# Dealing the modulation's products unevenly over the steps of a QR decomposition

## The chip, the cores and the metric

The kernel runs on one core of a Trainium2 chip. The metric is the device time of one execution in microseconds. Beside the timed runs there is one execution recorded by the hardware profiler; its span and the time lines below come from that one.

## What is computed

The input `x` has 8 samples of 512 tokens and 576 features, with one condition vector per sample. Two layers follow one another, all in float32.

```python
# layer 0: rotate each sample inside a 64-dimensional subspace
U, _ = jnp.linalg.qr(P)                       # P is 576 x 64
v = jax.nn.silu(cond) @ W.T + b               # entries of a skew 64 x 64 matrix A
R = expm(A)                                   # one per sample
z = jnp.einsum('btn,nd->btd', x, U)
x = x + jnp.einsum('btd,nd->btn', jnp.einsum('btd,bde->bte', z, R) - z, U)
# layer 1: a transformer block with modulation
ada = jax.nn.silu(c) @ ada_w + ada_b          # 8 x 3456
shift_msa, scale_msa, gate_msa, shift_mlp, scale_mlp, gate_mlp = jnp.split(ada, 6, axis=1)
x = x + gate_msa * attention(modulate(layernorm(x), shift_msa, scale_msa))
x = x + gate_mlp * mlp(modulate(layernorm(x), shift_mlp, scale_mlp))
```

The attention mixes the 16 heads of one token, and the MLP is 2304 wide.

## The kernel before

**The front of the kernel.** In the first 213 us the kernel makes the subspace, the rotations and the modulation. The QR of `P` is done by Householder steps, one for each of the 64 columns (`qr_step`, line 271, called from the loop at line 555). TensorE contributes two small products to each step: `rp` (line 274) broadcasts a row of the matrix, and `dp` (line 282) sums columns over the partitions. The rest of the step is a chain on VectorE: `sg` (line 291) reads `rp`, `w` (line 320) needs the norm `nrm` that ScalarE makes from `dp` (line 298), and then come the update of the matrix `m` (lines 327 and 337) and the products of the next column, `t` (lines 263 and 268). The next `rp` needs the updated `m`, and the next `dp` needs `t`.

**What is put beside it.** After each step (from the third on, line 558) the loop calls `next(side)` once. `side` is the generator `beside()` (line 528). Whatever it issues in that call stands in TensorE's queue behind the `dp` of this step and ahead of the `rp` of the next one. The order on TensorE, VectorE, ScalarE and GpSimd is the order in which the instructions are written here, since the stage has a manual schedule (line 164); SyncE's queue of DMAs is ordered by the scheduler.

`beside()` deals out three kinds of work:

- The entries of the skew matrices, `skew_entries` (line 399): eight groups of five products, four products per step, in steps 4 to 13.
- The modulation, `modulations()` (line 517): nine column blocks (`ada_columns`, line 360) of five products each (line 364, moving 384 columns over 8 rows of the condition), with a copy by ScalarE into `ada_rows` after each block (line 366) and the load of the block four further on. After blocks 1, 2, 5 and 7 a `modulation(v)` (line 371) transposes a part of `ada_rows` into `mod` by ten or twelve short products (lines 375 and 379) and ScalarE copies the result. A piece is what the generator does from one `yield` to the next: one column product, or one `modulation`; there are 49 pieces.
- The matrix exponential of all eight skew matrices, `expm` (line 445): the even and odd series by a few 64 x 64 products (`products`, line 424; eight per call, line 429), their sums on GpSimd, and 19 squarings of two `products` calls each, the last of one.

`expm` is itself a generator. In the version before it yields `True` or `False`: with `True`, `beside()` also takes one `next(rest)`, where `rest` is the modulation dealt in threes by `paced(3, ...)` (line 342); with `False` nothing is added. So steps 14 to 17 get three pieces each, then every step of the series gets three, the step with the products `hic` and `hin` (27) and the squarings (31 to 49) get none, and what is left follows in step 50.

```python
rest = paced(3, [modulations()])
...
for free in expm(*eyes):
    if free:
        next(rest, None)
    yield
for _ in rest:
    yield
```

When the generator's blocks 4 and 8 are complete, the gates are stored to DRAM by SyncE (line 369).

**Behind it.** From 213 us the triangular factor is inverted block by block, the first tile is rotated, and from then on the tiles go through qkv (line 821), attention on VectorE (lines 859 to 894), projection (line 957) and the MLP (lines 1001 to 1080).

Of the kernel before, what the change touches and what calls it, by code (L numbers as in the profile page):

```python
# [49 lines left out]
def rotate_then_dit_block(  # L50
# [113 lines left out]
    with tc.manual_schedule(engines=engines), tc.tile_pool(name="prep", bufs=1) as prep, tc.tile_pool(name="qrs", bufs=2) as qrs, tc.tile_pool(  # L164
# [177 lines left out]
        def paced(n, parts):  # L342

            k = 0
            for part in parts:
                for _ in part:
                    k += 1
                    if k % n == 0:
                        yield
# [6 lines left out]
        def load_ada(g):  # L356
            aws[g] = adap.tile([128, NK, AC], F32, tag="aw", name=f"aw_{g}")
            load_rows(aws[g], ada_w[:, g * AC : (g + 1) * AC], 65)

        def ada_columns(g):  # L360
            ps = ps_m.tile([B, AC], F32, tag="m", name=f"ada_{g}")
            for c in range(NK):
                k = srows(c)
                nc.tensor.matmul(ps, lhsT=sc[0:k, c, :], rhs=aws[g][0:k, c, :], start=c == 0, stop=c == NK - 1)  # L364
                yield
            nc.scalar.copy(ada_rows[:, g * AC : (g + 1) * AC], ps)
            for k in range(2):
                if g == (4, 8)[k]:
                    nc.sync.dma_start(out=gates_d[k], in_=ada_rows[:, (3 * k + 2) * D : (3 * k + 3) * D])

        def modulation(v):
            ps = ps_m.tile([128, NK, B], F32, tag="m", name=f"mod_{v}")
            for c, rows in enumerate(KROWS):
                first = v * D + c * 128
                nc.tensor.matmul(
                    ps[0:rows, c], lhsT=ada_rows[:, first : first + rows], rhs=ident[0:B, 0:B], start=True, stop=True
                )
            if v > 1:
                nc.tensor.matmul(
                    ps[64:128, 4],  # L380
                    lhsT=ada_rows[:, v * D + 512 : (v + 1) * D],
                    rhs=ident[0:B, 0:B],
                    start=True,
                    stop=True,
                )
            for c0, c1, rows in ((0, 4, 128), (4, 5, 128 if v > 1 else 64)):
                dst = mod[0:rows, v // 3 * 2 + v % 3, c0:c1, :]
                if v % 3:
                    nc.scalar.activation(dst, ps[0:rows, c0:c1], AF.Identity, bias=ones[0:rows, 0:1])
                else:  # L390
                    nc.scalar.copy(dst, ps[0:rows, c0:c1])
# [29 lines left out]
        def ex(tag):  # L421
            return exs.tile([128, B // 2, R], F32, tag=tag, name=f"ex_{tag}")

        def products(lhs, rhs, name):

            ps = ps_ex.tile([128, B // 2, R], F32, tag="ex", name=name)
            for b in range(B // 2):
                for p in (slice(0, R), slice(R, 128)):
                    nc.tensor.matmul(ps[p, b, :], lhsT=lhs[p, b, :], rhs=rhs[p, b, :], start=True, stop=True)
            return ps  # L430
# [14 lines left out]
        def expm(i1, i2, half):  # L445


            a, at_s = ex("a"), ex("at_s")
            nc.gpsimd.tensor_tensor(au, au, skew_mask.unsqueeze(1).to_broadcast([128, B // 2, R]), ALU.mult)
            yield True  # L450
            nc.scalar.copy(at_s, products(au, i1, "at"))
            nc.gpsimd.tensor_tensor(a, au, at_s, ALU.subtract)
            yield True
            yield True

            s1, s2, s3 = ex("s1"), ex("s2"), ex("s3")
            nc.scalar.copy(s1, products(a, a, "aa"))

            ns = prep.tile([128, B // 2], F32, tag="ns", name="ns")
            nan = prep.tile([128, B // 2], F32, tag="nan", name="nan")  # L460
            nc.vector.tensor_reduce(ns, a, AX.X, ALU.add, apply_absolute_value=True)
            nc.gpsimd.tensor_scalar(ns, ns, EXPM_LIMIT * 2.0**-N_SQUARINGS, None, ALU.is_ge)
            parts = {}
            for name, cs in (("c", COS_C), ("n", SIN_C)):
                lo, hi, tp = parts[name] = ex("lo" + name), ex("hi" + name), ex("tp" + name)
                nc.gpsimd.tensor_scalar(lo, s1, cs[1], None, ALU.mult)
                if name == "n":
                    nc.gpsimd.tensor_tensor(lo, lo, i1, ALU.add)
                nc.gpsimd.tensor_scalar(hi, i1, cs[3], None, ALU.mult)
            yield True  # L470
            nc.scalar.copy(s2, products(s1, s1, "ss"))
            ps = ps_m.tile([128, B // 2], F32, tag="m", name="over")
            nc.tensor.matmul(ps, lhsT=half, rhs=ns, start=True, stop=True)
            nc.scalar.copy(nan, ps)
            yield True
            nc.scalar.copy(s3, products(s1, s2, "sss"))
            for name, cs in (("c", COS_C), ("n", SIN_C)):
                lo, hi, tp = parts[name]
                for acc, s, c in ((hi, s1, cs[4]), (hi, s2, cs[5]), (lo, s2, cs[2])):
                    nc.gpsimd.tensor_scalar(tp, s, c, None, ALU.mult)  # L480
                    nc.gpsimd.tensor_tensor(acc, acc, tp, ALU.add)
            nc.gpsimd.tensor_scalar(nan, nan, 0.0, 3e38, ALU.is_gt, ALU.mult)
            nc.gpsimd.tensor_scalar(nan, nan, 3e38, 0.0, ALU.mult, ALU.mult)
            for _ in range(4):
                yield True
            for name in ("c", "n"):
                lo, hi, tp = parts[name]
                nc.scalar.copy(tp, products(s3, hi, "hi" + name))
                nc.gpsimd.tensor_tensor(lo, lo, tp, ALU.add)
            yield False  # L490
            yield True
            even, odd = parts["c"][0], parts["n"][0]
            e, f, e2, f2 = ex("e"), ex("f"), ex("e2"), ex("f2")
            sn = ex("sn")
            nc.scalar.copy(sn, products(a, odd, "sn"))
            nc.gpsimd.tensor_tensor(e, even, sn, ALU.subtract)
            nc.gpsimd.tensor_tensor(f, even, sn, ALU.add)
            nc.gpsimd.tensor_tensor(f2, f, i2, ALU.add)
            nc.gpsimd.tensor_tensor(e2, e, i2, ALU.add)
            yield True  # L500
            yield True

            for k in range(N_SQUARINGS):
                pair = [(e, e2, f2, f"pe_{k}"), (f, f2, e2, f"pf_{k}")]
                if k % 2:
                    pair.reverse()
                if k == N_SQUARINGS - 1:
                    pair = [x for x in pair if x[0] is f]
                made = [products(other, src, name) for src, _, other, name in pair]
                for (src, plus, _, _), ps in zip(pair, made):  # L510
                    nc.scalar.copy(src, ps)
                    if len(pair) == 2:
                        nc.gpsimd.tensor_tensor(plus, src, i2, ALU.add)
                yield False
            nc.gpsimd.tensor_tensor(fmi, f, nan.unsqueeze(2).to_broadcast([128, B // 2, R]), ALU.add)

        def modulations():

            for g in range(9):
                yield from ada_columns(g)  # L520
                if g + 4 < 9:
                    load_ada(g + 4)
                v = {1: 0, 2: 1, 5: 3, 7: 4}.get(g)
                if v is not None:
                    modulation(v)
                    yield

        def beside():
            yield
            yield  # L530
            yield from paced(4, [skew_entries(g) for g in range(8)])
            skew_rows()
            rest = paced(3, [modulations()])
            for _ in range(4):
                next(rest)
                yield
            for free in expm(*eyes):
                if free:
                    next(rest, None)
                yield  # L540
            for _ in rest:
                yield
# [8 lines left out]
        first_xt = xin.tile([128, D], F32, tag="xt", name="xt_0_0", bufs=2)  # L551
        eyes = identities()
        side = beside()
        t, done = column_products(0), None
        for j in range(R):
# [687 lines left out]
    for k, (b, ts) in enumerate(units):  # L1243
# [38 lines left out]
        s3s, rest = mlp(pr, gate_m, aside)  # L1282
# [58 lines left out]
```

## Time and profile before

| | |
|---|---|
| median of 3 runs | 2154.73 us |
| lowest and highest | 2151.36 and 2156.78 us |
| the profiled execution | 2156.77 us |
| its span, first to last instruction | 2155.1 us |
| TensorE busy | 2051.7 us, 95% |
| VectorE busy | 1818.1 us, 84% |
| GpSimd busy | 730.3 us, 34% |
| ScalarE busy | 432.9 us, 20% |
| chain that ended last | 75% on TensorE, 16% on VectorE |

Times in the profile are counted from the start of the span. The page has the span in 40 slices with the busy share of each engine in tenths and the TensorE clock that was granted, then the chain that ended last, then the groups of instructions by line. PE is TensorE, DVE is VectorE, ACT is ScalarE, POOL is GpSimd, SP is SyncE. In a timeline row stand the start, the time of the row, engine, line, operation, output and inputs, shapes, how many, and in brackets how long the engine was idle before and what ended that. In a row of waits stand the waiting instruction, the one that released it, the time in all, the number and the longest.

A step is counted here from one `sg` (line 291) to the next, with the first column as step 0. Step 14 begins at 56.6 us, step 17 at 66.3, step 27 at 107.1, step 31 at 124.8, step 50 at 181.7, and the last at 213.1.

### The profile page before, as it was taken

The numbers are of one execution on the slowest core, as the hardware profiler recorded it, in microseconds if no ns is written. First come the engines' busy times: TensorE is split into PE (matmuls) and PEld (weight loads), VectorE is DVE, ScalarE is ACT, GpSimd is POOL, SyncE is SP. The second block draws the span as 40 slices with busy tenths as digits, with TensorE's granted clock in tenths as the row PEclk, the third lists the DMA queues.
The fourth block names the chain that finished last, engine by engine and source line by source line (L and its number), as shares of the span: only waits on it lengthen the run. The fifth ranks groups of instructions, "written<-read, shape, count | busy, mean of one in ns | idle before, by whom it ended". The sixth has DMA issues, their size and how long they took to land.

```text
span 2155.1 us, 28246 instructions
## 1 busy us (share of the span) xinstructions
PE 2051.7 (95%) x10109; PEld 1621.1 (75%) x10109; DVE 1818.1 (84%) x2548; ACT 432.9 (20%) x1040; POOL 730.3 (34%) x959
## 2 busy tenths in 40 slices
PE   5996898999999999999999999999999999998998
PEld 3476666777878878887878787888878787776777
DVE  8898499799997988979797979798997999989821
ACT  2232222221211221222121121121121211111210
POOL 2331153241523333333333243323333434343322
PEclk9855799999999999999999999999999999999999
DMA  8202256375757666575748484756657676665564
GB/s 278 87 2 75 82 189 176 116 227 167 216 192 205 210 185 213 170 236 161 249 137 270 127 266 147 223 194 195 221 177 222 194 226 166 205 188 189 168 193 139
DMA packets 251456, 392.44 MB, mean 182 GB/s; under 512 B 86926, under 2 KB 139099, under 8 KB 251316
## 3 DMA queue, kind: packets, MB, share of 16 engines
q1 hardware_dynamic: 225396, 364.09, 54.9%
q10 hardware_dynamic: 25920, 26.55, 3.6%
q8 instruction: 80, 1.31, 0.2%
q14 instruction: 60, 0.49, 0.1%
HBM read 331.63 MB, written 58.94 MB: 181 GB/s over the span
## 4 chain that ended last, share of the span: by engine, by line
PE 75%; DVE 16%; issue 3%; POOL 2%; DMA 2%; ACT 2%; ACTq 0%; SPq 0%; POOLq 0%; DVEq 0%
PE fc L1001 25%; PE qkvp L821 15%; PE fc L1075 9%; PE fc L1080 6%; PE pj L957 5%; DVE sc L866 3%; PE fc L1077 3%; PE p L1106 2%; DVE qk L859 2%; PE ada L364 1%; PE rot L762 1%; PE zps L751 1%; DVE att L894 1%; DVE pv L887 1%; PE dp L282 1%
## 5 line engine op out<-in xcount | busy, mean ns | idle before, releaser
L1001 PE MATMUL fc<-h2T,w 128*128 128x256 f32 x2304 | 519.0, 381 | 3.4 <-ACT h2T L977 2.3
L821 PE MATMUL qkvp<-wqkv,hT 128*128 128x288 f32 (+1 forms) x1920 | 484.4, 409 | 7.5 <-ACT qs L832 5.3
L1001 PEld LDWEIGHTS fc<-h2T,w 128*128 128x128 f32 x2304 | 433.6, 191 | 70.9 <-ACT h2T L977 9.5
L821 PEld LDWEIGHTS qkvp<-wqkv,hT 128*128 128x128 f32 (+1 forms) x1920 | 363.0, 191 | 110.0 <-ACT qs L832 7.1
L859 DVE TENSOR_TENSOR qk<-qkv 128x2304 f32<-128x2304 f32 x128 | 336.7, 2631 | 4.2 <-ACT qkv L829 2.0
L887 DVE TENSOR_TENSOR pv<-sc,qkv 128x2304 f32<-128x2304 f32 x128 | 333.5, 2606 | 2.7
L894 DVE TENSOR_REDUCE att<-pv 128x144 f32<-128x2304 f32 x128 | 326.0, 2547 | 3.1
L866 DVE TENSOR_REDUCE sc<-qk 128x64 f32<-128x2304 f32 x128 | 326.2, 2548 | 2.5
L1100 POOL TENSOR_TENSOR s<-gt 128x128 f32<-128x128 f32 x144 | 88.9, 619 | 453.3 <-ACT gt L1022 453.3
L1022 ACT ACTIVATE gt<-fc,b 128x256 f32<-128x256 f32 x288 | 118.8, 471 | 610.1 <-PE fc L1001 575.2
L1075 PE MATMUL fc<-wq,gt 128*128 128x288 f32 x576 | 170.8, 417 | 9.9 <-ACT gt L1022 6.7
L1080 PEld LDWEIGHTS fc<-wt,ss 128*128 128x128 f32 x1152 | 161.2, 191 | 15.3
L1080 PE MATMUL fc<-wt,ss 128*128 128x144 f32 x1152 | 165.1, 287 | 0.0
L1033 POOL TENSOR_TENSOR x<-x,mt 128x288 f32<-128x288 f32 x64 | 71.6, 1120 | 227.3 <-DVE mt L1032 227.3
L832 ACT COPY qs<-qkvp 128x288 f32<-128x288 f32 x180 | 71.5, 397 | 378.4 <-PE qkvp L821 337.9
L1097 POOL TENSOR_TENSOR ss<-gt 128x128 f32<-128x128 f32 x144 | 116.9, 812 | 69.6 <-PE fc L1080 68.0
L1099 POOL TENSOR_TENSOR ss<-gt,ss 128x128 f32<-128x128 f32 x144 | 133.0, 924 | 10.0
L1075 PEld LDWEIGHTS fc<-wq,gt 128*128 128x128 f32 x576 | 99.4, 190 | 44.4 <-issue 15.6
L957 PE MATMUL pj<-w2q_p,aT 128*128 128x288 f32 x384 | 104.0, 406 | 2.9 <-DVE u L1137 1.6
L146 POOL TENSOR_TENSOR rstd_m<-rstd_m,mhalf 128x1 f32<-128x1 f32 x32 | 26.7, 835 | 222.1 <-DVE rstd_m L145 222.1
L1075 PE MATMUL fc<-wt,gt 128*128 128x288 f32 x288 | 93.9, 408 | 0.0
L1077 PE MATMUL fc<-wq,ss 128*128 128x288 f32 x288 | 93.9, 408 | 0.0
(265 smaller groups left out, 2379.9 us busy)
## 6 DMA issues: line engine op xcount, KB each, us to landing
w<-in_fc_w SPq DMA_DIRECT2D x288, 256.0 KB, 5.0
wq<-in_fc_q SPq DMA_DIRECT2D x144, 432.0 KB, 4.3
wt<-comb_d SPq DMA_DIRECT2D x144, 432.0 KB, 5.6
tok<-qs ACTq DMA_DIRECT2D x180, 144.0 KB, 1.8
qkv<-tok SPq DMA_DIRECT2D x30, 864.0 KB, 4.6
w2q_p<-in_proj_w SPq DMA_DIRECT2D x32, 432.0 KB, 4.0
xT<-in_x_t SPq DMA_DIRECT2D x16, 640.0 KB, 4.9
w1t<-in_fc_t SPq DMA_DIRECT2D x80, 128.0 KB, 4.4
```

Source lines behind the costliest of these rows:

```text
L821: nc.tensor.matmul(ps, lhsT=hT[0:k, c, i * 128 : (i + 1) * 128], rhs=wqkv[0:k, c, cols], start=c == 0, stop=c == NK - 1,)
L859: nc.vector.tensor_tensor(pr, q[:, c * HC : (c + 1) * HC].unsqueeze(2).to_broadcast([128, HC, H, DH]), k.unsqueeze(1).to_broadcast([128, H ...
L866: nc.vector.tensor_reduce(sc[t][:, c * HC : (c + 1) * HC, :], pr, AX.X, ALU.add)
L887: nc.vector.tensor_tensor(pr, sc[t][:, c * HC : (c + 1) * HC, :].unsqueeze(2).to_broadcast([128, HC, DH, H]), v.unsqueeze(1).to_broadcast( ...
L894: nc.vector.tensor_reduce(att[:, c * HC : (c + 1) * HC, :], pr, AX.X, ALU.add)
L957: nc.tensor.matmul(ps, lhsT=aT[0:k, c, :], rhs=w, start=c == 0, stop=c == NK - 1)
L1001: nc.tensor.matmul(bank[:, k], lhsT=lhs, rhs=h2T[rows, c, 0 : NU * 128], start=start, stop=stop, skip_group_check=True)
L1022: nc.scalar.activation(gt[:, k].rearrange("p t s -> p (t s)"), bank[:, k], AF.Gelu, bias=b1[:, 2 * g + k : 2 * g + k + 1])
L1075: nc.tensor.matmul(p[k], lhsT=whole[k][0], rhs=whole[k][1], start=g == 0, stop=stop)
L1077: nc.tensor.matmul(p[2], lhsT=whole[2][0], rhs=whole[2][1], start=g == 0, stop=stop)
L1080: nc.tensor.matmul(bank[:, side], lhsT=lhs, rhs=rhs[:, n * QUARTER : (n + 1) * QUARTER], start=False, stop=stop, skip_group_check=True,)
L1099: nc.gpsimd.tensor_tensor(ss[:, 2], gt[:, 1, 0], ss[:, 1], ALU.subtract)
```

## The change

`expm` now yields a number instead of a truth value, and `beside()` takes that many single pieces of the modulation in that step. Steps of the series without products yield 4, those with products 1, and the step with `hic` and `hin` and the squarings still 0. The first four steps take three pieces each as before. After `expm`, what is left is taken one piece at a time.

```diff
             a, at_s = ex("a"), ex("at_s")
             nc.gpsimd.tensor_tensor(au, au, skew_mask.unsqueeze(1).to_broadcast([128, B // 2, R]), ALU.mult)
-            yield True
+            yield 4
             nc.scalar.copy(at_s, products(au, i1, "at"))
             nc.gpsimd.tensor_tensor(a, au, at_s, ALU.subtract)
-            yield True
-            yield True
+            yield 1
+            yield 4
...
                 nc.gpsimd.tensor_scalar(hi, i1, cs[3], None, ALU.mult)
-            yield True
+            yield 1
             nc.scalar.copy(s2, products(s1, s1, "ss"))
...
             nc.scalar.copy(nan, ps)
-            yield True
+            yield 1
             nc.scalar.copy(s3, products(s1, s2, "sss"))
...
-            for _ in range(4):
-                yield True
+            yield 1
+            for _ in range(3):
+                yield 4
             for name in ("c", "n"):
...
-            yield False
-            yield True
+            yield 0
+            yield 4
...
             nc.gpsimd.tensor_tensor(e2, e, i2, ALU.add)
-            yield True
-            yield True
+            yield 1
+            yield 4
...
-                yield False
+                yield 0
...
-            rest = paced(3, [modulations()])
+            rest = modulations()
             for _ in range(4):
-                next(rest)
+                for _ in range(3):
+                    next(rest)
                 yield
-            for free in expm(*eyes):
-                if free:
+            for n in expm(*eyes):
+                for _ in range(n):
                     next(rest, None)
                 yield
```

## The prediction

> **What bounds the kernel now.** I read the slices of the page first, then the waits of the stretch that the change touches, then that stretch step by step.
>
> In the slices of the page each figure covers 54 us; the change works in the second and third of the 40.
>
> ```profile
> PE   5996898999999999999999999999999999998998
> DVE  8898499799997988979797979798997999989821
> PEclk9855799999999999999999999999999999999999
> ```
>
> From about 230 us on TensorE is full at full clock and the change moves nothing there. In the first 213 us VectorE leads: the 64 columns of the QR go one after another, and each step is a chain of some 20 VectorE instructions with two small products (rp, dp) from TensorE. There the clock is half at times. A microsecond saved or lost in a step moves everything behind it, since the QR ends before the first tile can be rotated.
>
> The next view gives busy time by stage; shown are steps 17 to 31 (which hold all the changed steps but four) and the squarings behind them.
>
> ```profile
> 66.28:128.66 62.38, 57.07 (x322) 26.48 (x320) 50.89 (x272) 14.70 (x55) 22.43 (x30) 0.78 0.19 58
> 128.66:181.66 53.00, 52.20 (x634) 48.57 (x633) 51.72 (x318) 20.99 (x71) 24.12 (x35) 0.50 0.01 2
> ```
>
> After the stretch and its length stand TensorE, its weight loads and VectorE: VectorE is busy for 50.89 of 62.38 us, so **11.5 us idle in steps 17 to 31**; some 0.5 of it is seams (a step without a wait, 59.81 to 63.06, shows 3.16 busy of 3.25). About 11.0 us is all that any order of these pieces can win here: 0.5% of the kernel. Who it waits for, in the list of waits of that stretch:
>
> ```profile
> DVE sg L291 <- PE rp L274: 9.3, 8, 1.7
> ```
>
> Eight steps begin late because rp stands in TensorE's queue behind the pieces put in front of it. How late depends on the clock. Below are the modulation products (L364) in two steps, from the timeline: step 15 at full clock, step 20 at half.
>
> ```profile
> 63.11 2.10 PE L364 MATMUL ada<-aw,sc 128*8 128x384 f32 x6
> 65.14 0.42 PE L274 MATMUL rp<-m,ident 128*128 128x47 f32 x2
> 66.00 0.39 PE L282 MATMUL dp<-t,ones 128*128 128x47 f32 x2 [0.45 <-DVE av L306]
> ```
>
> ```profile
> 79.78 3.94 PE L364 MATMUL ada<-aw,sc 128*8 128x384 f32 x6
> 83.65 0.42 PE L274 MATMUL rp<-m,ident 128*128 128x43 f32 x2
> ```
>
> A product is two records, so three pieces are six records. Warm they are spaced 0.322 us ((65.14 - 63.11 - 0.10 of gap)/6), cold 0.640 ((83.65 - 79.78)/6, less the seam). Warm, three pieces end 0.9 us before dp can start, hidden. Cold, they push rp late and VectorE idles.
>
> The clock follows how much TensorE did in the 3.41 us before. The next view cuts the stretch at the clock's own changes and counts L364 alone; its first pair is TensorE busy and records, the granted clock is the third from the end.
>
> ```profile
> 63.05:66.47 3.42, 2.25 (x7) 0.55 (x8) 1.00 0.84 278
> 66.47:69.88 3.41, 1.48 (x4) 0.10 (x2) 1.00 0.46 119
> 69.88:73.29 3.41, 3.35 (x6) 0.65 (x6) 0.50 0.38 143
> 73.29:76.71 3.42, 1.20 (x4) 0.10 (x2) 1.00 0.03 6
> 76.71:80.12 3.41, 1.79 (x3) 0.20 (x4) 0.50 0.83 259
> 80.12:83.53 3.41, 3.41 (x6) 0.55 (x4) 0.50 0.00 0
> 83.53:86.95 3.42, 2.30 (x7) 0.46 (x6) 1.00 0.09 9
> ```
>
> Read each row's load with the next row's clock: a warm window with six or seven records stays warm, one with four turns cold; a cold window with six turns warm, one with three stays cold. Windows of products alone (107.43 to 110.84, no record) turn cold too.
>
> **The change part by part.** Same instructions, other places. The 49 pieces (45 column products, four transposed modulations) were dealt three at a time; steps 14 to 17 still get three. I count them out:
> - steps 18, 20, 24, 25, 28: four products each (eight records);
> - step 19: the at products and modulation 1; steps 21, 22, 23, 29: the products of the series and one product each;
> - step 26: modulation 3 first, then three products; step 30: two products, modulation 4, one product;
> - step 27 none; steps 50 to 53: one each, where before step 50 had one.
>
> Added and removed: nothing. The dealing loop around them emits no instruction.
>
> **Warm price of a four-piece step:** 8 x 0.322 = 2.58 us, plus 0.67 from the last record through rp and dp to the next fill (65.04 to 66.33, less the wait for dp): 3.25 us, against 2.9 to 3.6 of VectorE. Nearly hidden. **Cold:** 8 x 0.640 = 5.12 plus 1.0 for rp and dp (step 19: 78.77 to 79.78): 6.1 us. Between them, if the clock turns inside the step: about one cold window with 5.3 records, 2.7 warm records, the end: 3.41 + 0.87 + 0.7 = 5.0. I take 5.4 for a step that follows a light one. Every four-piece step but 25 follows a light window, and light steps have at most 2 records of L364: by the rows above they leave the clock cold.
>
> Now VectorE's wait by step, step length less VectorE's busy time of before:
> - 18: 4.18 of before plus two warm records 0.64, less 3.17: 1.65 (before 1.0)
> - 19: one piece for three, at products 0.61, then the wait for two copies on ScalarE (0.37 + 0.47) and ten short records; VectorE 3.61: 0 to 0.9, take 0.2 (before 1.8)
> - 20: 5.4 - 3.12 = 2.3 (before 1.5); 21 to 23: 0 (before 0.2)
> - 24: 5.4 - 3.6 = 1.8 (before 0.6); 25: 3.25 - 3.37, 0 (before 1.6)
> - 26: two short records, a wait for the copy of the row (nrm 0.26, nsg 0.28, copy 0.47 stand in ScalarE's order before it), eight more, then six of L364: 4.5 warm, 7.5 cold, less 2.96: 1.5 to 4.6, take 2.4 (before 0.1)
> - 28: 5.4 - 2.91 = 2.5 (before 1.25); 29: 0 (before 0.9)
> - 30: four records, modulation (12 short records, 1.3 warm), two records, end: 3.9 warm, 7.0 cold, less 2.86: 1.0 to 4.2, take 2.6 (before 1.95)
> - 50 to 53: a cold piece takes 1.45 us (181.89 to 183.34) and rp there came when m was ready: 0 to 0.1 each, 0.2 in all.
>
> Sum 13.65 against 11.0: **+2.7 us**.
>
> *Moved past queues.* SP holds its first load of the next stage for the last piece (the wait of L1048 on L364, 87.7 us, over at 183.41). That piece moves from step 50 to 53, 10 to 15 us later, and the second gates store to step 54. The next thing SP does is a 44.9 us wait until 237.8, and the first reader of those loads (L1051) starts at 253.9: hidden; with the cover gone it would cost at most those 15 us. The ada loads were issued from 85.7 to 93.0 and used 20 us later; one step more or less is covered. GpSimd's long run after ss starts in the same step and has until step 27: covered.
>
> The same sum by the Trainium skill: "TensorE: Matmul & The Clock Gate", Part 1, says the clock falls only after about 3.4 us of idle. By that the light steps would not cool it, and all heavy steps would cost their warm price. The rows above (four records in a window, no idle, clock 0.50 next) speak against it here, so the trace decides.
>
> The profiled execution took 2156.77 us for a span of 2155.1. 2156.77 + 2.7 = 2159.4; I say **2159.0**. That execution lies 2.0 above the median of the three runs (2154.73; they go from 2151.36 to 2156.78), so against the median it is +4.3 us, 0.2%. The windows of the clock need not lie alike against the steps from run to run, and I read the 5 us of spread that way; the sum is for windows that lie unluckily in about half of the steps.
>
> **Rivals.**
> - *The four-piece steps keep the clock warm* (2.58 us of 3.25 is load enough, if a window holds no light step): waits left are 0.1 to 0.4 each in 18, 20, 28, and the modulations' 1.5 in 26 and 1.0 in 30, some 4 in all, 7.0 less than now: 2149.8 us. For: six records kept it warm from 56 to 66 us. Against: no two heavy steps are neighbours but 24 to 26. Chance 0.10; of it a third is faster than by 0.3% (6.5 us, about what a measurement of this kernel can tell from no change).
> - *All heavy steps stay cold to their end* (place: the seven steps; price: 6.1 us, and 7.5 and 7.0 for 26 and 30): 2.9 + 0.9 + 3.0 + 2.5 + 0.3 + 4.6 + 3.2 + 4.2 = 21.6, 10.6 over before: 2167 us. It decides from the point where a cold window holds fewer than five records, because it is cut by the light step before. For: 76.71 to 83.53 was cold twice running. Chance 0.25 together with lesser forms that still pass 2161.2.
> - *The change does nothing:* what 19, 21 to 23, 25 and 29 save is what 18, 24, 26 and 30 pay: 2155 to 2157. This is the forecast's lower half.
>
> **How the numbers follow.** Likeliest: waits of 9 to 16 us, 2155 to 2161, chance 0.65. Warm rival 0.10, cold rival 0.25. Range: 2151 to 2166 leaves out the ends of both. Within 0.3% of 2154.73 (2148.3 to 2161.2): 0.65 + 0.07 = 0.72, less the part of the forecast that passes its upper bound, 0.04: 0.68. Slower 0.29, faster 0.03.
>
> **What would show it.** In the profile after: clock 0.50 in part of steps 18, 20, 24, 28 and 30; steps 21, 22, 23 and 29 without a wait before L291; the longest wait of L291 in step 26 or 30, behind a modulation; the wait of L291 for rp at 11 to 14 us in fewer, longer pieces; the stage behind the QR unchanged in length. Wrong it would be if the clock stays 1.00 from step 18 to 30, if light steps still wait, or if the stages behind 213 us change.

## The result, and the profile after

The changed kernel takes **2163.2 us** in the median of 7 runs (2160.3 to 2166.18), against 2154.73 (2151.36 to 2156.78, now 7 runs): a ratio of 1.004, with a 95% interval of 1.0031 to 1.005. It is 8.5 us slower. The time lies inside the range that was given, but past the bound of 0.3% that the forecast put its main chance on; 0.29 had been given to that. The profiled execution took 2163.45 us, for a span of 2161.7.

The same views as before. First the busy tenths and the clock on the page of the changed kernel.

```profile
PE   6997898999999999999999999999999999997998
...
PEclk9765699999999999999999999999999999999999
```

From the seventh slice to near the end nothing has changed. In the first five the clock's digits are others, but digits of 54 us tell little. The stage view for steps 18 to 31 (in step numbers, since the times have moved) stands in the next fence: the kernel before, then the changed one, each in its first profile.

```profile
69.89:128.66 58.77, 53.66 (x304) 24.55 (x302) 47.37 (x254) 13.55 (x50) 21.70 (x29) 0.76 0.17 55
```

```profile
71.88:133.86 61.98, 56.02 (x298) 27.14 (x296) 46.59 (x254) 13.43 (x50) 20.62 (x28) 0.70 0.16 52
```

The stretch is 3.2 us longer, with six TensorE records fewer (three products have gone to the tail). VectorE does the same 254 instructions. The mean clock fell from 0.76 to 0.70. The wait that makes it, in the list of waits:

```profile
DVE sg L291 <- PE rp L274: 13.1, 7, 3.1
```

It was 9.3 us in eight pieces of at most 1.7: now there are fewer and longer ones, because the pieces stand in fewer steps. Counted by step (step length less VectorE's busy time), the waits of steps 18 to 31 are 14.9 us, against 10.95. The short seams between instructions, which steps without a wait show too, are left out of such sums here and below; with them the two rows above give 15.4 and 11.4.

Three steps of the changed kernel show the three cases. The timeline of TensorE has step 20, a four-piece step behind a light one:

```profile
80.66 5.29 PE L364 MATMUL ada<-aw,sc 128*8 128x384 f32 x8
85.88 0.42 PE L274 MATMUL rp<-m,ident 128*128 128x43 f32 x2
```

Eight records take 5.2 us, 0.65 each: cold to the end, and VectorE waits 2.85 us. Step 28 has the same eight records, with the clock full:

```profile
118.24 2.75 PE L364 MATMUL ada<-aw,sc 128*8 128x384 f32 x8
120.92 0.41 PE L274 MATMUL rp<-m,ident 128*128 128x35 f32 x2
```

They end after 2.7 us, and the wait is 0.18 us. Step 26 begins with a modulation:

```profile
108.19 0.38 PE L375 MATMUL mod<-ident,ada_rows 8*128 8x8 f32 x2
109.14 1.09 PE L375 MATMUL mod<-ident,ada_rows 8*128 8x8 f32 x7 [0.57 <-ACT ada_rows L366]
...
110.27 3.54 PE L364 MATMUL ada<-aw,sc 128*8 128x384 f32 x6
113.74 0.41 PE L274 MATMUL rp<-m,ident 128*128 128x37 f32 x2
```

TensorE stands idle for 0.57 us until the row's copy is made, does short records, and the six records (three products) behind them are cold again (3.54 us where warm ones take 2.10): 3.15 us of wait.

The clock by its own windows, cut as in the view of before, with the records of L364 alone:

```profile
68.80:72.21 3.41, 1.35 (x4) 0.19 (x4) 1.00 0.59 163
72.21:75.62 3.41, 3.41 (x7) 0.82 (x6) 0.50 0.27 99
75.62:79.04 3.42, 0.74 (x3) 0.00 (x0) 1.00 0.41 107
79.04:82.45 3.41, 1.79 (x3) 0.38 (x4) 0.50 0.42 157
82.45:85.86 3.41, 3.41 (x6) 0.55 (x4) 0.50 0.00 0
85.86:89.28 3.42, 0.90 (x3) 0.10 (x2) 1.00 0.11 13
89.28:92.69 3.41, 1.21 (x2) 0.10 (x2) 0.50 0.72 249
92.69:96.10 3.41, 1.42 (x3) 0.10 (x2) 0.50 0.00 0
96.10:99.52 3.42, 2.44 (x5) 0.51 (x5) 0.50 0.00 0
99.52:102.93 3.41, 3.11 (x5) 0.41 (x3) 0.50 0.15 18
102.93:106.35 3.42, 2.78 (x5) 0.66 (x6) 0.50 0.71 246
106.35:109.76 3.41, 1.34 (x4) 0.18 (x2) 1.00 0.02 5
109.76:113.17 3.41, 2.90 (x5) 0.65 (x6) 0.50 0.00 0
113.17:116.59 3.42, 0.64 (x2) 0.00 (x0) 1.00 0.00 0
116.59:120.00 3.41, 1.76 (x6) 0.54 (x7) 1.00 0.01 2
```

Here the change is seen at work. A light step lets the clock fall behind the windows at 75.6 to 79.0 (step 19, with the at products and a modulation) and at 85.9 to 89.3 (step 21, with products of the series and two records). Steps 22 and 23 are light too, the clock stays at half for 17 us, and steps 24 and 25 pay for it. It turns full at 106.35, just in time to meet the modulation of step 26, and falls again. The window from 113.17, which holds two records and the 32 of hic and hin, did not cool it: that is why step 28 came cheap.

### The profile page after: what moved, and what is told of

Same layout as the page of the kernel before. It is cut to its first block, busy times and chain, and to the rows that moved or that the text cites. A ratio compares the mean times of both kernels' runs of the same rounds, so it can differ in the third digit from the quotient of the medians.

```text
span 2161.7 us, 28246 instructions
## 1 busy us (share of the span) xinstructions
PE 2059.7 (95%) x10109; PEld 1624.2 (75%) x10109; DVE 1818.3 (84%) x2548; ACT 432.7 (20%) x1040; POOL 727.4 (34%) x959
## 3 DMA queue, kind: packets, MB, share of 16 engines
q1 hardware_dynamic: 225396, 364.09, 54.7%
q8 instruction: 80, 1.31, 0.2%
## 4 chain that ended last, share of the span: by engine, by line
PE 74%; DVE 15%; issue 3%; POOL 3%; DMA 2%; ACT 1%; ACTq 0%; SPq 0%; POOLq 0%; DVEq 0%
PE fc L1003 25%; PE qkvp L823 15%; PE fc L1077 9%; PE fc L1082 5%; PE pj L959 5%; DVE sc L868 4%; PE fc L1079 3%; DVE qk L861 3%; PE p L1108 2%; PE ada L364 2%; PE rot L764 1%; PE zps L753 1%; PE dp L282 1%; DVE att L896 1%; PE rp L274 1%
## 5 line engine op out<-in xcount | busy, mean ns | idle before, releaser
L1102 POOL TENSOR_TENSOR s<-gt 128x128 f32<-128x128 f32 x144 | 89.3, 622 | 454.4 <-ACT gt L1024 454.4
```

## The experiments

Each run's time is compared with runs of the kernel before on the same chip, which there took 2156.9 to 2159.7 us in the median, 2 to 5 us more than in the first measurement. So ratios are compared, not times.

Two theories came out of the prediction, and two more were held against them.

- **Clock:** light steps let the clock fall, and the full step behind them is run at half.
- **Crowding:** four pieces are too many for a step, at any clock.
- **Modulation:** the transposes at the head of step 26 and inside step 30 carry the loss.
- **Tail:** the pieces left for step 50 and later delay what comes after the QR.

### Each half of the change alone

`ones_only` keeps the ones and gives three pieces where the change has four; `fours_only` keeps the fours and gives three where the change has one. The edit is the same at each such place; one is shown.

```diff
-            yield 4
+            yield 3
```

> Half of the change: one piece in steps with products, still three in the others, the rest one at a time from step 50. The clock theory (light steps let the clock fall, and the next full step pays for it): waits of VectorE in steps 18 to 31 of some 9.5 us (about 1 in 18 and 24, 2 to 3 in 20 and 28 where a modulation sits, 1.5 in 30), so 5 us less than the changed kernel: about 2157.5. The crowding theory (four pieces are too many for a step at any clock): as the kernel before or a little better, 2152 to 2155, with no step over 1 us. The tail theory (pieces from step 50 on delay what comes after the QR): slower than the changed kernel, since eleven pieces instead of four are left for it.

Measured: ratio 1.0008 (0.9999 to 1.0018). Steps 18 to 31 in the stage view:

```profile
70.30:127.28 56.98, 49.56 (x274) 25.35 (x272) 47.29 (x254) 12.17 (x46) 21.37 (x29) 0.69 0.18 58
```

The waits of steps 18 to 31 are 8.9 us, with 2.93 in step 20, 1.31 in 24 and 3.13 in 28. The tail (steps 50 to 62) is 32.2 us long against 31.5; the 0.7 is steps 55 and 56, where the last modulation fell. The tail theory is out: eleven pieces stood there, seven more than in the changed kernel, and the kernel is not slower than the changed one but faster (1.0008 against 1.004).

```diff
-            yield 1
+            yield 3
```

> The other half: four pieces in steps without products, still three in those with, nothing left for step 50. The clock theory: no light step but 27, 29 and 30, so steps 20 to 25 stay mostly warm; waits of 10 to 12 us, the modulations' steps 19, 24, 26 and the step 28 behind the light 27 the longest: about 2159. The crowding theory: every four-piece step pays 2 us or more, as in the changed kernel: 2163 or more. The tail theory: 2155 or less, as nothing is left for the tail.

Measured: ratio 1.0006 (0.9995 to 1.0018). Steps 18 to 31:

```profile
69.46:124.54 55.08, 47.59 (x306) 24.14 (x305) 47.06 (x255) 13.90 (x51) 20.56 (x28) 0.84 0.19 61
```

The waits are 7.4 us, less than I had expected, the most of them in steps 18 (1.66) and 28 (2.67), where the clock was cold in part. Steps 20 and 25, with four column products, wait 0.12 us and nothing. Four pieces are not too many while the clock is full: crowding is out as well. Where one of the four is a modulation (steps 24 and 26), the wait is 0.8 us even at full clock. Each half alone measures less than 0.1% (the intervals reach 0.18%) and both together 0.4%. That fits a loss made by a light step with a full one behind it; the runs with idle work put it to the test.

### Keeping the clock up in the light steps

`after_heat` adds idle products (their result is read by nobody) to the light steps of the changed kernel; `mods_late` takes the modulations out of the stretch; `mods_late_heat` does both.

```diff
+        def heat(n):
+            for _ in range(n):
+                nc.tensor.matmul(heater, lhsT=sc[:, 0, :], rhs=wqkv[:, 0, 0:AC], start=True, stop=True)
...
-            for n in expm(*eyes):
+            for at, n in enumerate(expm(*eyes)):
+                if n < 4 and at < 12:
+                    heat(2 if n else 3)
```

> The changed kernel with idle work in its light steps: two products of the modulation's shape into a PSUM tile that nobody reads in steps 19, 21, 22, 23 and 29, three in step 27. The output is not touched. The clock theory: the clock stays full through steps 20 to 30 but for those with a modulation; steps 20, 24 and 28 fall from 2.8, 2.8 and 0.2 us of wait to under 0.5, 26 to some 1.9, 30 to some 1.3: waits of 6 to 8 us instead of 15, about 2156. The crowding theory: no step gets shorter, and the light ones grow by up to 1 us each: 2163 to 2168. The modulation theory (the transposes at the head of step 26 and inside step 30 carry the loss, whatever the clock): at most 2 us less, 2161.

Measured: ratio 1.0003 (0.9993 to 1.0013), so TensorE was given more to do and the kernel became faster than the changed one (1.004). Steps 18 to 31:

```profile
71.24:128.75 57.51, 53.67 (x324) 25.13 (x322) 47.73 (x254) 13.31 (x50) 21.75 (x29) 0.88 0.18 56
```

Steps 20, 24 and 25 wait 0.13 us and nothing, as expected. The 9.2 us that are left, more than the 6 to 8 expected, lie for the most part behind modulations: 1.72 in step 18, behind the modulation of step 17, and 3.75 and 2.23 in steps 26 and 27, behind the modulation at the head of step 26; the idle products of step 27 were themselves cold there.

```diff
-                v = {1: 0, 2: 1, 5: 3, 7: 4}.get(g)
-                if v is not None:
-                    modulation(v)
-                    yield
+            for v in (0, 1, 3, 4):
+                modulation(v)
+                yield
```

> The changed kernel with the four modulations dealt last (steps 50 to 53) and no idle work: what the modulations alone cost. The clock theory: four pieces behind light steps stay dear without the idle work; waits in steps 18 to 31 of about 9 us (2 to 2.9 each in 20, 24 and 28 or 30), against 0.6 with it, and 2.2 in the tail: ratio to before about 1.002. The modulation theory: waits as with the idle work, about 1 us, ratio 0.998.

Measured: ratio 1.001 (0.9998 to 1.0023), 9.4 us of waits, as the clock theory has it. Without modulations and without idle work, steps 20, 24, 28 and 30 still wait 1.73, 2.03, 3.28 and 1.35 us.

> As the run with idle work, and the four modulations dealt after the 45 column products, in steps 50 to 53, so that steps 14 to 30 hold column products alone. The clock theory: full clock from step 5 to step 30, under 0.4 us of wait in each step, 2 in all; each modulation in the cold tail costs about 0.6: waits of 4 to 5 us, about 2152, below the kernel before. The crowding theory: 2160 or more. The modulation theory: 5 to 6 us less than the changed kernel, 2157.

Measured: ratio **0.9984** (0.9974 to 0.9994), waits of 0.6 us in steps 18 to 31, below the 2 expected. The same stretch in the view by stage, `mods_late` first and `mods_late_heat` below it:

```profile
69.71:126.41 56.70, 49.51 (x270) 21.33 (x268) 46.68 (x255) 12.40 (x44) 21.24 (x29) 0.76 0.18 59
```

```profile
71.28:120.67 49.39, 45.85 (x296) 20.12 (x294) 47.90 (x255) 12.41 (x44) 21.57 (x29) 0.99 0.21 66
```

With 26 more records on TensorE the stretch is 7.3 us shorter; the clock (third from the end) is 0.99 instead of 0.76. The two kernels differ in the idle products alone (they ran on two chips, each beside the kernel before, and their intervals don't overlap). This pair shows the cause: it is the granted clock and not the number of pieces in a step. The modulations alone (from the changed kernel to `mods_late`) are worth 0.3%, against 0.26% for the idle work behind that: both count. How much of the modulations' part runs through the clock was not separated.

### Even dealing, and a version that beats both

If uneven dealing is what cools the clock, even dealing with the modulations out of the way should need no idle work. `even_mods_late` deals threes in steps 14 to 29 (none in 27), then the modulations in steps 50 to 53. `even_halves` cuts each modulation in two; `even_halves_heat` adds idle products in steps 2, 3 and 27.

> Three pieces in every step of the series but 27 and 30, modulations last: the evenness of the version before, without the transposes among the products and without idle work. The clock theory: clock full to step 27, one cold step behind it (28, about 1.3 us), waits of under 2 us in steps 18 to 31, 2.2 in the tail: ratio about 0.998. The crowding theory has nothing against it. The modulation theory: the same as its neighbour with four and one, so the difference of these two runs is the clock's.

Measured: ratio 0.9995 (0.9984 to 1.0007), above the 0.998 expected. Steps 18 to 27 wait 0.2 us in all, but the light step 27 costs more than I had thought: 2.00 us in step 28 and 2.74 in step 29, where 1.3 was expected for the two. The tail takes 33.65 us, 2.2 more than before, as expected. Against its neighbour with four and one, `mods_late` on the same chip, the median is 2158.24 us to 2161.75, and the ratio of the means 0.9984 (0.9976 to 0.9993): the evenness alone is worth some 0.16%, and the modulations, which stand at the same place in both, can't be the reason.

```diff
+                if c == 1:
+                    yield
...
+            yield
...
+            for v in (0, 1, 3, 4):
+                yield from modulation(v)
```

> As the run before, with each modulation cut in two pieces, dealt over steps 50 to 57. A half takes about 1.1 us cold and should end before rp is due: the tail's 2.2 us of waits fall to 0.2, ratio about 0.997. If the tail stays as long, it is the ScalarE copies of the modulations that delay nrm and not TensorE.

Measured: ratio 0.9979 (0.9967 to 0.999). The stage view of steps 50 to 62 shows the tail of `even_mods_late`, and then that of `even_halves`:

```profile
175.64:209.29 33.65, 22.21 (x98) 20.90 (x97) 27.37 (x183) 7.48 (x35) 0.46 (x1) 0.50 0.34 119
```

```profile
175.06:206.58 31.52, 23.49 (x98) 21.50 (x97) 27.03 (x184) 7.48 (x35) 0.47 (x1) 0.50 0.38 127
```

The same 98 TensorE records fit without any wait beyond those of the kernel before (31.5 us, as there) when no step has a whole modulation; so it was TensorE, and not ScalarE's copies.

```diff
+            heat(6, ident, sc[:, 0, :])
             yield
+            heat(6, ident, sc[:, 0, :])
             yield
...
+                if at == 9:
+                    heat(3, wqkv[:, 0, 0:AC], sc[:, 0, :])
```

> As the run before, with idle products of 128 columns in steps 2 and 3 and three of the modulation's shape in step 27 (their results are read by nobody). The clock theory: the clock is full from step 4 or 5 on in every execution, so steps 4 to 13 take 34.6 us (34.6 to 36.2 were seen), and step 28 loses its wait: 1 to 2 us less than the run before, ratio about 0.9962. If the first rise of the clock does not depend on TensorE's load, steps 4 to 13 stay as scattered.

Measured: **2151.01 us against 2159.67, ratio 0.9963** (0.995 to 0.9976), the best of all. Steps 18 to 31:

```profile
69.71:117.79 48.08, 41.58 (x276) 20.09 (x274) 46.55 (x255) 12.29 (x44) 21.05 (x28) 0.95 0.22 68
```

The waits of steps 18 to 31 are 0.4 us. In this one profile the clock rises at 17.8 us, where it rose at 24.7 to 31.3 in the other profiles, and steps 4 to 13 take 34.15 us, the least of all profiles (34.45 to 36.2).

### Both kernels again

Between profiles the clock's windows fall at other places, so I took two more of each kernel.

> The kernel before, unchanged, for a second profile with the clock's windows lying differently against the steps. If the place of the windows makes the spread of the runs, its waits in steps 18 to 31 differ from the 10.95 us of the first profile by 2 us or more, towards 4 to 9 us, with the same steps behind a fall of the clock; if the spread comes from elsewhere, they are within 1 us of it. Ratio 1.000.

> The kernel before once more, for a third place of the windows: waits of 4 to 12 us in steps 18 to 31.

> The changed kernel, unchanged, on the same chip as the run above: waits in steps 18 to 31 of 12 to 16 us by the clock theory (14.9 in its first profile), some 4 to 8 more than the kernel before; ratio 1.003 to 1.004.

> The changed kernel once more, for a third place of the windows: waits of 11 to 17 us in steps 18 to 31; step 28 cold this time with 2 us or more if the first profile's 0.18 was the luck of a window.

Steps 18 to 31 in the stage view: `before_again`, `before_third`, `after_again` and `after_third`, in this order.

```profile
70.43:123.86 53.43, 47.87 (x304) 23.36 (x302) 48.06 (x254) 13.55 (x50) 21.42 (x29) 0.86 0.19 61
```

```profile
69.74:122.65 52.91, 47.49 (x304) 22.67 (x303) 47.56 (x254) 13.54 (x50) 21.72 (x29) 0.87 0.19 62
```

```profile
70.11:129.25 59.14, 52.85 (x298) 26.20 (x296) 46.55 (x255) 13.43 (x50) 20.62 (x28) 0.74 0.18 58
```

```profile
69.26:127.69 58.43, 51.44 (x298) 25.82 (x297) 47.20 (x254) 13.33 (x50) 21.34 (x28) 0.76 0.18 58
```

The waits of the kernel before are 4.7 and 4.7 us here, not 10.95: the first profile had caught it with the clock at 0.76 in this stretch, and these have it at 0.86 and 0.87. I had expected the same steps behind a fall of the clock, and they aren't: step 18 waits 1.0 us in the first and third profile and not in the second; step 28 waits in all three. The waits of the changed kernel are 12.0 and 10.6 us against 14.9 (10.6 is just under the 11 to 17 expected of the third). In the third its heavy steps 20, 24 and 25 wait 0.07, 0.05 and nothing, while step 28 waits 3.27 us instead of 0.18, and step 30 4.03: which step pays is the luck of the windows, and that some pay is not.

The timed ratios were 1.0007 (0.9996 to 1.0018) for the unchanged copy and 1.0046 (1.003 to 1.0062) for the changed kernel, a little above the 1.003 to 1.004 expected. In the 35, 33 and 17 timed runs of the kernel before beside these experiments, time and granted clock over the span go together, with correlations of -0.85, -0.86 and -0.91. That says that the spread goes with the clock, not in which stage.

## Why the prediction was right in its mechanism and short in its size

**The sum of the changed kernel held.** I had 13.65 us of waits; the three profiles have 14.9, 12.0 and 10.6, 12.5 in the mean. By step, the first profile against the forecast: 18: 1.71 (1.65); 19: 0 (0.2); 20: 2.85 (2.3); 21 to 23: 0.5 (0); 24: 2.77 (1.8); 25: 0.93 (0); 26: 3.15 (2.4); 28: 0.18 (2.5); 29: 0 (0); 30: 2.42 (2.6). The list of waits was to show 11 to 14 us in fewer, longer pieces, and it shows 13.1 in seven instead of 9.3 in eight (10.5 in six and 9.2 in four in the two later profiles). The prices held: the warm four-piece step 28 took 3.24 us on TensorE up to the next fill (3.25 forecast), the cold step 20 took 5.79 (eight records at 0.640 and 0.67 for the end make 5.79). That the sum came so near is partly luck: steps 20, 24, 25 and 26 cost 3.2 us more than forecast and step 28 2.3 less, as the windows fell.

**The term that was mis-sized is the 11.0 us that were taken away from it.** "Sum 13.65 against 11.0" used the waits of one profiled execution for the kernel before. I had seen that it lies 2.0 us above the median and that the windows lie differently from run to run, and allowed no more than those 2.0 us for it. Two more profiles of the same kernel have 4.7 us each, so the mean is 6.8, and the difference is 12.5 - 6.8 = 5.7 us, not 2.7. These are means of three profiles that spread by 4 and 6 us. The uneven dealing was slow in all three profiles, the even one in one of three, and that was the one that I had.

**Figures of the working that don't follow from their rows.** The step without a wait has 0.09 us of seams, so 15 steps have 1.35 and not 0.5; the same amount stands on both sides of the difference. The cold rival put 0.3 us into its sum for step 25, where its price of 6.1 less 3.37 is 2.7, so it would have come to 24.0 us and not 21.6. And TensorE is at full clock from 244 us in that profile, not from 230. None of this enters the +2.7.

**Where the difference lies,** from the three profiles of each (mean spans 2160.5 and 2154.0, 6.5 us apart): steps 18 to 31 +4.8 us (59.9 against 55.0), all ahead of them +0.4, steps 32 to 62 +0.1, behind the QR +1.2. The 4.8 is less than the 5.7 of waits because VectorE's own time in the stretch is 0.9 us shorter (46.8 against 47.7).

**The moved transfers were hidden**, as forecast. The first of the held loads on SP went from 183.41 to 196.63 us, the first qkv product starts within 0.3 us of its old distance from the end of the QR in the three pairs of profiles, and steps 50 to 53 wait exactly as before (0.11 and 0.28 us; I had allowed 0.2 in all).

**The rivals.** The warm rival took place step by step and never for a whole run: step 28 in two profiles, 20, 24 and 25 in the third. The cold one came nearest in steps 24 to 26 of two profiles (2.8, 0.9 and 3.15 us, where it had 2.5, 0.3 and 4.6). The page "TensorE: Matmul & The Clock Gate", Part 1, has the clock fall only after an idle window. That would have made this change nearly free. These traces have it fall after windows with three or four records of L364 and the small products (behind 66.47 to 69.88 of the kernel before, where TensorE was idle for 0.2 us), and stay up when idle products fill them (0.99 in `mods_late_heat`).

**What stays open.** The timed medians differ by 8.5 us here and by 9.9 on another chip (interval 6.5 to 13.4), the profiled spans by 6.1 to 6.7. The executions profiled again lie at the lower end of their timed runs (2154.39 of 2154.39 to 2163.86, and 2161.04 of 2161.04 to 2171.7), so the upper end has no trace. The 1.2 us behind the QR (1.1, 1.0 and 1.5 in the pairs) can't be laid to the change: that stretch takes 1941.9 to 1946.6 us in the three profiles of the kernel before, and 1941.9 to 1950.1 in all 14. It goes with the time that the clock stands at half in it (54.7 to 69.3 us, correlation 0.87), so a part of the spread from run to run lies there and not in the QR.

**How much work keeps the clock up.** The number of L364 records alone doesn't say it. Five records and 3.11 us of L364 in the cold window at 99.5 us of the changed kernel did not turn it warm, five with 2.78 us in the next one did, and the two records beside hic and hin from 113.17 on kept it full, where hic and hin alone (107.43 to 110.84 of the kernel before) did not. But the records don't all use the same number of the 128 rows: the last record pair of each block has 65, hic, hin and the series 64, a modulation 8. I counted all TensorE records in the 368 windows between steps 4 and 31 of the 14 profiles, from the first rise of the clock on, each with the time of its columns (0.322 us for 384 at full clock, 0.640 at half) times its share of the rows. At half clock, the 40 windows with up to 0.745 of their length filled stayed there and the 33 from 0.766 on rose; at full clock the 39 up to 0.352 fell and the 252 from 0.39 on stayed, with four between that did either. In work this is one bound: what 3.7 to 4.1 full records of 384 columns do in 3.41 us. The windows above fit (0.70 at 99.5 us, 0.87 in the next, 0.39 at 113.17, 0.21 for hic and hin alone). It was read from the traces afterwards; no run varies the rows alone.

## What to carry to other kernels

When small work is tucked into the waits of another engine's chain, deal it so that TensorE's load is even: a step that is spared lets the clock fall, and the next step pays double for its pieces (0.65 us a record against 0.32). Put work that cannot keep the clock up (the modulation's short records of 8 rows behind a copy) where a cold clock is covered, in pieces that fit a cold step. And before subtracting a wait that one profile shows, take the kernel's profile a second time: here the same kernel had 4.7 us of it or 10.95.

## What the runs showed that I had not expected

Idle products made the kernel faster: 26 more records on TensorE in steps 18 to 31 shortened them from 56.7 to 49.4 us. Twelve idle records in each of steps 2 and 3 went with a first rise of the clock at 17.8 us, where the 13 other profiles have it between 24.7 and 31.3. And a single light step (27) cost 4.7 us over the next two steps (2.00 and 2.74) when it ended a stretch that had been at full clock for 78 us.
